# Cross-attention on one core: the last two blocks' subtraction split over VectorE and GpSimd, their inverse sums spread by DMA, their PSUM banks and step order changed

## The chip, the core and the metric

The kernel runs on one core of a Trainium2 chip. The metric is the device time of one execution in microseconds (us); lower is better. Engines are named as in the profile: PE (TensorE), DVE (VectorE), ACT (ScalarE), POOL (GpSimd), and SP, whose queue issues nearly all DMAs.

## What is computed

The reference is a cross-attention layer in float32. 16 batches of 1024 rows of 512 features attend to 64 context rows each, with 16 heads of 32 features:

```python
xq  = ada_ln(x, cond, Wss_q)          # layernorm, then scale and shift from silu(cond)
xkv = ada_ln(ctx, cond, Wss_kv)
q = (xq @ Wq + bq)                    # 16 heads x 32
k, v = split(xkv @ Wkv + bkv)
scores = einsum("bqhd,bkhd->bhqk", q, k) / sqrt(32)
attn = softmax(scores, axis=-1)
out = einsum("bhqk,bkhd->bqhd", attn, v)
return x + (out @ Wp + bp)
```

## The kernel before

The 16 x 1024 rows are cut into 32 blocks of 512 rows (`NB = 32`, two to a batch). Queries, scores and results are held transposed, features over the 128 partitions. The three 512x512 products use a seven-product scheme (Strassen's kind): `query_product(i, n)` and `product(i, n)` are the seven products of the query projection and of the output projection, and `added(i, n)` adds each product's accumulator to the residual rows `r`.

A block passes these steps, each of them a helper:

- `scores(i, z)`: PE makes the scores of context half `z` (0 or 1) in two PSUM pairs `ps`; DVE takes the column maxima into `m`, ACT copies the scores to the SBUF tile `s` (128x2048).
- `maxima(i)`: DVE joins the maxima of both halves and spreads them with a 32x32 block transpose to `mb` (128x2048). `subtract(i)`: POOL forms `s - mb`, once for each half. `weights(i, z)`: ACT takes the exponential in place.
- The sums: `total` (POOL adds the halves) and `row_total` (DVE), or, for the last block, `sums(i, z)` on DVE for each half and `halves_total`. `inverse_rows(i)`: DVE takes the reciprocal of the small 128x64 tile `lt`; SP writes it to a DRAM tile `ltd` and reads it back rearranged in four small DMAs to `vr` (128x64). `spread_rows(i)`: DVE spreads `vr` by a block transpose to `vb` (128x2048).
- `mix(i)`: PE multiplies the exponentials with the values into the PSUM tiles `po`; half 0 comes first. `divided(i)`: DVE forms `ot = po * vb`.
- The output projection: `biased` (ACT puts the bias into the PSUM accumulators `pp`), `row_sums` (POOL forms the sums of `ot` that the seven products need), seven `product`s on PE and seven `added`s on DVE, and the DMAs of the result out.

The program calls these helpers in an order written out by hand; every engine runs its own instructions in that order, and semaphores hold an instruction until what it needs is there. A loop handles the blocks up to 29; the *way out*, a written list after it, handles the last two, called `y` (block 30) and `z` (block 31). In the way out block 29 (`y - 1`) is projected without the seven products: `project(y - 1, t)` for four row tiles `t`, each of four PE instructions into one PSUM bank, and `projected(y - 1, t)`, which adds it to the rows on DVE and stores them.

Four PSUM banks (0 to 3) serve the projections. `ring` is the list from which `project` takes its bank in turn, `ks` in `mix(y - 1, ks=(2, 3, 1, 0))` are the banks of the four `po` tiles of block 29, and `acc_bank(i, n)` gives the banks of the accumulators. A bank that is taken again is held until the last reader of its old content is done. The other four banks are the two pairs in which the scores and the `po` of `y` and `z` stand in turn. Bank numbers before: `ring = [1, 0]`; block 30's accumulators are in banks 2 and 3 (its second product in 1), block 31's in 0 and 1 (its second product in 3).

## Time and profile before

| | |
|---|---|
| time, median of 3 runs | 1018.12 us (1017.64 to 1018.77) |
| time of the profiled execution, and its span | 1018.0 us, 1016.1 us |
| PE busy | 1002.6 us, 99% of the span |
| DVE, POOL, ACT busy | 861.7 us (85%), 809.3 us (80%), 638.5 us (63%) |
| granted PE clock | full speed over the span, but for the last few us |

The profile is of one execution. Its times run from the span's start; the way out begins near 940 us. In the timeline a row is a group of equal instructions: start, length, engine, line, operation, output<-inputs, count, and in square brackets how long the engine sat idle before it and who ended that. Ends of PE's groups are modelled, and a group's length reaches a little past the start of the next one.

### The profile page before, as it was taken

Reading aid. Unit: us, or ns where it says so; the run is one execution under the profiler, and the core shown is the slowest. Engines: PE = TensorE matmul, PEld = TensorE weight load, DVE = VectorE, ACT = ScalarE, POOL = GpSimd, SP = SyncE. Lnnn points to the kernel's source line nnn. Section 1 sums busy time; section 2 is a strip of 40 time slices with the busy share of each in tenths; the row PEclk is TensorE's granted clock in tenths of the full one; section 3 lists DMA queues with packets and bytes.
Section 4 is the critical chain, followed back from the end, with each engine's and each line's share of the span. In section 5 each row is a group of like instructions: output and inputs, shape, how many; then the busy total and the mean of one; then the engine's idle time right before and its main releaser. Section 6 shows DMA issues by size and latency. Waiting matters only on the chain.

```text
span 1016.1 us, 21264 instructions
## 1 busy us (share of the span) xinstructions
PE 1002.6 (99%) x8096; PEld 766.6 (75%) x8096; DVE 861.7 (85%) x1184; ACT 638.5 (63%) x1025; POOL 809.3 (80%) x518
## 2 busy tenths in 40 slices
PE   7999999999999999999999999999999999999998
PEld 6888777777777777777777777877777777777746
DVE  6687888898889888988898888889888888876785
ACT  3787566666667666666666666766666666665520
POOL 3668998888898888888988888898888888987781
PEclk9999999999999999999999999999999999999999
DMA  9664564444455544444554354444544444335122
GB/s 301 250 173 126 145 195 133 123 137 149 156 155 164 168 127 128 128 153 151 160 167 138 120 167 126 149 161 158 167 134 123 150 131 156 116 122 169 44 77 96
DMA packets 112101, 149.82 MB, mean 147 GB/s; under 512 B 34008, under 2 KB 45296, under 8 KB 112000
## 3 DMA queue, kind: packets, MB, share of 16 engines
q1 hardware_dynamic: 111600, 147.69, 46.9%
q8 instruction: 64, 1.05, 0.4%
q0 software_dynamic: 256, 0.52, 0.2%
q14 instruction: 37, 0.30, 0.1%
q10 hardware_dynamic: 144, 0.26, 0.1%
HBM read 79.21 MB, written 34.60 MB: 112 GB/s over the span
## 4 chain that ended last, share of the span: by engine, by line
PE 89%; DMA 3%; DVE 2%; POOL 2%; SPq 2%; issue 1%; ACT 1%; DVEq 0%; POOLq 0%; ACTq 0%
PE pq L551 36%; PE pp L964 35%; PE po L838 7%; PE ps L670 6%; PE pp L865 1%; PE pv_B L551 1%; PE pk_B L551 1%; SPq L398 1%; DMA x<-in_x_dram 1%; DMA w_v_sb<-in_L_xcond_Wkv_dram 1%; DMA b_v_sb<-in_L_xcond_bkv_dram 1%; PE pv_A L551 1%; POOL s L729 1%; DVE m L687 1%; POOL sum L769 0%
## 5 line engine op out<-in xcount | busy, mean ns | idle before, releaser
L729 POOL TENSOR_TENSOR s<-s,mb 128x2048 f32<-128x2048 f32 x64 | 290.5, 4565 | 124.3 <-DVE mb L716 124.3
L696 ACT COPY s<-ps 128x1024 f32<-128x1024 f32 x128 | 129.6, 1012 | 103.9 <-DVE m L687 61.7
L687 DVE TRANSPOSE_TENSOR_REDUCE m<-ps 128x32 f32<-128x1024 f32 x128 | 150.7, 1214 | 31.9 <-PE ps L670 31.9
L964 PE MATMUL pp<-w_p_sb,ot 128*128 128x256 f32 x736 | 169.1, 379 | 1.3 <-DVE ot L818 0.9
L987 DVE TENSOR_TENSOR r<-pp,r 128x512 f32<-128x512 f32 x210 | 136.7, 671 | 29.9 <-PE pp L964 24.5
L964 PEld LDWEIGHTS pp<-w_p_sb,ot 128*128 128x128 f32 x736 | 139.7, 190 | 21.3 <-issue 1.7
L590 ACT ACTIVATE qt<-pq,bias_t 128x256 f32<-128x256 f32 x256 | 105.7, 464 | 78.6 <-PE pq L551 78.5
L735 ACT ACTIVATE s<-s 128x2048 f32<-128x2048 f32 x64 | 122.3, 1913 | 47.3 <-POOL s L729 47.3
L769 POOL TENSOR_TENSOR sum<-s,s 128x2048 f32<-128x2048 f32 x31 | 140.7, 4540 | 3.1 <-ACT s L735 3.1
L964 PEld LDWEIGHTS pp<-WT,s 128*128 128x128 f32 x496 | 89.5, 189 | 57.8 <-issue 26.8
L551 PE MATMUL pq<-xt_sums,w_q_sums 128*128 128x256 f32 x512 | 123.7, 385 | 0.0
L964 PE MATMUL pp<-WT,s 128*128 128x256 f32 x496 | 123.1, 391 | 0.5 <-DVE r L987 0.5
L551 PEld LDWEIGHTS pq<-xt_sums,w_q_sums 128*128 128x128 f32 x512 | 95.0, 190 | 35.2 <-issue 22.5
L551 PE MATMUL pq<-xt,w_q_sb 128*128 128x256 f32 x512 | 121.3, 380 | 0.0
L551 PE MATMUL pq<-xt,w_q_sums 128*128 128x256 f32 x512 | 121.0, 379 | 0.0
L964 PE MATMUL pp<-WT,ot 128*128 128x256 f32 x496 | 117.3, 379 | 0.0
L551 PEld LDWEIGHTS pq<-xt,w_q_sb 128*128 128x128 f32 x512 | 97.0, 190 | 15.6 <-issue 1.7
L551 PEld LDWEIGHTS pq<-xt,w_q_sums 128*128 128x128 f32 x512 | 97.2, 190 | 13.3
L964 PEld LDWEIGHTS pp<-WT,ot 128*128 128x128 f32 x496 | 94.2, 190 | 13.6 <-issue 0.8
L347 ACT ACTIVATE x<-x,rstdq 128x512 f32<-128x512 f32 x128 | 97.1, 808 | 3.1 <-POOL rstdq L322 3.1
L456 ACT ACTIVATE xt<-xt,ss_q 128x512 f32<-128x512 f32 x124 | 94.1, 808 | 2.3 <-DMA out_dram<-r 1.3
L304 DVE BATCH_NORM_STATS2 bs<-x 128x6 f32<-128x512 f32 x128 | 87.1, 680 | 4.1 <-DMA x<-in_x_dram 4.1
(174 smaller groups left out, 1481.0 us busy)
## 6 DMA issues: line engine op xcount, KB each, us to landing
x<-in_x_dram SPq DMA_DIRECT2D x32, 1024.0 KB, 5.4
r<-in_x_dram SPq DMA_DIRECT2D x32, 1024.0 KB, 5.3
xt<-ht SPq DMA_DIRECT2D x488, 64.0 KB, 2.0
out_dram<-r SPq DMA_DIRECT2D x60, 512.0 KB, 3.7
wss_kv<-in_L_xcond_Wss_kv_dram SPq DMA_DIRECT2D x4, 512.0 KB, 8.3
wss_q<-in_L_xcond_Wss_q_dram SPq DMA_DIRECT2D x4, 512.0 KB, 8.0
vr<-ltd SPq DMA_DIRECT2D x128, 8.0 KB, 1.6
out_dram<-r SPq DMA_DIRECT2D x7, 256.0 KB, 2.3
```

Source lines behind the costliest of these rows:

```text
L304: nc.vector.bn_stats(bs, r)
L347: nc.scalar.activation(dst, src, AF.Identity, bias=rstd[:, 1, j : j + 1], scale=rstd[:, 0, j : j + 1])
L456: nc.scalar.activation(xt[:, :, c, :], xt[:, :, c, :], AF.Identity, scale=ss["q"][:, c, b : b + 1], bias=ss["q"][:, NC + c, b : b + 1],)
L551: nc.tensor.matmul(out_, lhsT=lhsT, rhs=rhs, start=new and m == 0 and c == 0, stop=c == HC - 1, skip_group_check=True,)
L590: nc.scalar.activation(dst, src, AF.Identity, bias=bq_t[:, o : o + 1])
L687: nc.vector.tensor_reduce(m_tiles[i][:, z, 2 * e : 2 * e + 2, :], s_banks[i, z][e].rearrange("p r (j a) -> p r j a", a=32), AX.X, ALU.max, ...
L696: nc.scalar.copy(s_tiles[i, z][:, 2 * e : 2 * e + 2, :], s_banks[i, z][e])
L729: eng.tensor_tensor(s_tiles[i, z], s_tiles[i, z], mb_tiles[i], ALU.subtract)
L735: nc.scalar.activation(p, p, AF.Exp, scale=SCALE)
L769: nc.gpsimd.tensor_tensor(t, s_tiles[i, 0], s_tiles[i, 1], ALU.add)
L964: nc.tensor.matmul(acc[products_of(i, n)][:, t * HO : (t + 1) * HO], lhsT=rows[:, c, t * P : (t + 1) * P], rhs=cols[:, c, :], start=n == 2 ...
L987: nc.vector.tensor_add(r, a, r)
```

## The change

The change concerns the way out alone; the 30 blocks before it are issued as before. Lines after it stand 15 to 17 lines later in the file where a helper moved.

```diff
+    def inverse_spread(i, lt):
+        turned_lt = small.tile([P, 2, 32], F32, tag="vr", name=f"vr_{i}")
+        nc.vector.transpose(turned_lt.rearrange("p h a -> p (h a)"), lt)
+        d = dram.tile([2, NC, 32, 32], F32, tag="lt", name=f"ltd_{i}")
+        nc.sync.dma_start(d.rearrange("h c x a -> (c x) h a"), turned_lt)
+        t = qpool.tile([P, NC, TB], F32, tag="vb", name=f"vb_{i}", bufs=1)
+        for r in range(HPC):
+            row = d[r // 2].rearrange("c (r j) a -> r c (j a)", r=2)[r % 2]
+            nc.sync.dma_start(
+                t[32 * r : 32 * r + 32], row.unsqueeze(0).to_broadcast([32, NC, TB])
+            )
+        vb_tiles[i] = t
+
     def inverse_rows(i):
         lt = lt_tiles.pop(i)
         nc.vector.reciprocal(lt, lt)
+        if i >= NB - 2:
+            inverse_spread(i, lt.rearrange("p r j -> p (r j)"))
+            return
...
     def acc_bank(i, n):
         if n == 2 and i >= NB - 2:
-            return 1 if i == NB - 2 else 3
-        return (2 if n in (1, 6, 5, 3) else 3) - (2 if i == NB - 1 else 0)
+            return 2 if i == NB - 2 else 1
+        return (2 if n in (1, 6, 5, 3) else 3) - (2 if i == NB - 2 else 0)
...
-    ring[:] = [1, 0]
+    ring[:] = [2, 3]
...
-    subtract(z)
+    subtract(z, nc.vector, (1,))
...
+    subtract(z, zs=(0,))
...
-    spread_rows(y)
...
-    spread_rows(z)
```

For blocks 30 and 31 the small tile of inverse sums is turned on DVE, written to DRAM, and read back by four DMAs, each of which fills 32 partitions of the full tile `vb` (256 KB each, 1 MB together) by reading the same rows 32 times. `subtract` of block 31 is made by DVE for half 1 and by POOL for half 0. Project tiles 0 to 3 of block 29 go to banks 2, 3, 2, 3 in place of 1, 0, 1, 0; block 30's accumulators to 0 and 1 (second product 2), block 31's to 2 and 3 (second product 1).

The steps of the way out stand in a new order; three places follow. On PE, from the projection of block 29 on (`pp_29`), before:

```order
L865 MATMUL pp_29_0_8778<-w_p_sb_102,ot_29_8744 128x512 x4
L865 MATMUL pp_29_1_8797<-w_p_sb_102,ot_29_8744 128x512 x4
L865 MATMUL pp_29_2_8804<-w_p_sb_102,ot_29_8744 128x512 x4
L838 MATMUL po_30_0_8818<-s_30_0_8572,V_B_123 32x512 x8
L838 MATMUL po_30_1_8819<-s_30_0_8572,V_B_123 32x512 x8
L838 MATMUL po_30_0_8818<-s_30_1_8606,V_B_123 32x512 x8
L838 MATMUL po_30_1_8819<-s_30_1_8606,V_B_123 32x512 x8
L865 MATMUL pp_29_3_8853<-w_p_sb_102,ot_29_8744 128x512 x4
L964 MATMUL pp_30_1_8746<-w_p_sb_102,ot_30_8858 128x256 x4
L964 MATMUL pp_30_2_8870<-w_p_sb_102,ot_30_8858 128x256 x4
L838 MATMUL po_31_0_8879<-s_31_0_8697,V_B_123 32x512 x8
```

and after:

```order
L882 MATMUL pp_29_0_8788<-w_p_sb_102,ot_29_8744 128x512 x4
L882 MATMUL pp_29_1_8802<-w_p_sb_102,ot_29_8744 128x512 x4
L855 MATMUL po_30_0_8809<-s_30_0_8572,V_B_123 32x512 x8
L855 MATMUL po_30_1_8810<-s_30_0_8572,V_B_123 32x512 x8
L855 MATMUL po_30_0_8809<-s_30_1_8607,V_B_123 32x512 x8
L855 MATMUL po_30_1_8810<-s_30_1_8607,V_B_123 32x512 x8
L882 MATMUL pp_29_2_8843<-w_p_sb_102,ot_29_8744 128x512 x4
L882 MATMUL pp_29_3_8848<-w_p_sb_102,ot_29_8744 128x512 x4
L855 MATMUL po_31_0_8863<-s_31_0_8703,V_B_123 32x512 x8
L855 MATMUL po_31_1_8864<-s_31_0_8703,V_B_123 32x512 x8
```

Block 30's `mix` now stands between project tiles 1 and 2, and block 31's `mix` (`po_31`, half 0 first) follows project tile 3 at once; block 30's first two products, which stood before it, come after it.

On DVE, from block 30's row sums (`lt_30`) to block 30's division, before:

```order
L774 TENSOR_REDUCE lt_30_8776<-sum_30_8702 128x64
L878 TENSOR_TENSOR r_29_8436<-pp_29_0_8778,r_29_8436 128x512
L789 RECIPROCAL lt_30_8776<-lt_30_8776 128x64
L707 TENSOR_REDUCE m_31_8793<-m2_31_8696 128x64
L716 STREAM_TRANSPOSE mb_31_8795<-m_31_8793 128x2048
L878 TENSOR_TENSOR r_29_8436<-pp_29_1_8797,r_29_8436 128x512
L800 STREAM_TRANSPOSE vb_30_8813<-vr_30_8786 128x2048
L878 TENSOR_TENSOR r_29_8436<-pp_29_2_8804,r_29_8436 128x512
L818 TENSOR_TENSOR ot_30_8858<-po_30_0_8818,vb_30_8813 128x1024
```

and after:

```order
L774 TENSOR_REDUCE lt_30_8753<-sum_30_8682 128x64
L687 TENSOR_REDUCE m2_31_8702<-ps_31_1_0_8755 128x32
L687 TENSOR_REDUCE m2_31_8702<-ps_31_1_1_8756 128x32
L803 RECIPROCAL lt_30_8753<-lt_30_8753 128x64
L789 STREAM_TRANSPOSE vr_30_8779<-lt_30_8753 128x64
L895 TENSOR_TENSOR r_29_8436<-pp_29_0_8788,r_29_8436 128x512
L707 TENSOR_REDUCE m_31_8795<-m2_31_8702 128x64
L716 STREAM_TRANSPOSE mb_31_8797<-m_31_8795 128x2048
L729 TENSOR_TENSOR s_31_1_8773<-s_31_1_8773,mb_31_8797 128x2048
L895 TENSOR_TENSOR r_29_8436<-pp_29_1_8802,r_29_8436 128x512
L895 TENSOR_TENSOR r_29_8436<-pp_29_2_8843,r_29_8436 128x512
L835 TENSOR_TENSOR ot_30_8856<-po_30_0_8809,vb_30_8783 128x1024
```

The row sums go ahead of block 31's last two maxima, the large transpose to `vb` is gone, a small one to `vr` is new, and the subtraction of half 1 stands ahead of the addition that empties project tile 1's bank.

On POOL, in the same stretch, before:

```order
L729 TENSOR_TENSOR s_30_0_8572<-s_30_0_8572,mb_30_8625 128x2048
L729 TENSOR_TENSOR s_30_1_8606<-s_30_1_8606,mb_30_8625 128x2048
L769 TENSOR_TENSOR sum_30_8702<-s_30_0_8572,s_30_1_8606 128x2048
L365 TENSOR_TENSOR r_29_8436<-r_29_8436,b_p_sb_101 128x512 x4
L729 TENSOR_TENSOR s_31_0_8697<-s_31_0_8697,mb_31_8795 128x2048
L729 TENSOR_TENSOR s_31_1_8771<-s_31_1_8771,mb_31_8795 128x2048
```

and after:

```order
L365 TENSOR_TENSOR r_29_8436<-r_29_8436,b_p_sb_101 128x512 x4
L729 TENSOR_TENSOR s_30_0_8572<-s_30_0_8572,mb_30_8635 128x2048
L729 TENSOR_TENSOR s_30_1_8607<-s_30_1_8607,mb_30_8635 128x2048
L769 TENSOR_TENSOR sum_30_8682<-s_30_0_8572,s_30_1_8607 128x2048
L729 TENSOR_TENSOR s_31_0_8703<-s_31_0_8703,mb_31_8797 128x2048
```

The bias additions to block 29's rows (`residual(y - 1)`) move ahead of block 30's subtraction, and one subtraction of block 31 is gone. In the list of steps at the end, block 31's `added(z, 2)` and its DMA move from after the fifth product to after the third.

84 lines of the change are left out of this document (42 added, 42 removed).

## The prediction

> **What bounds the kernel now.** I read the page first (engines, chain), then PE's timeline of the way out, then those of DVE, POOL, ACT and SP in the same window. The page's rows of busy time and of the chain that ended last:
>
> ```profile
> PE 1002.6 (99%) x8096; PEld 766.6 (75%) x8096; DVE 861.7 (85%) x1184; ACT 638.5 (63%) x1025; POOL 809.3 (80%) x518
> PE 89%; DMA 3%; DVE 2%; POOL 2%; SPq 2%; issue 1%; ACT 1%; DVEq 0%; POOLq 0%; ACTq 0%
> ```
>
> PE is the bound. The change removes no matmul, so it can only win time in which PE stands still in the way out. PE's timeline there:
>
> ```profile
> 965.72 1.25 PE L670 MATMUL ps<-qt,K_B 32*32 32x512 f32 x32
> 967.65 10.57 PE L865 MATMUL pp<-w_p_sb,ot 128*128 128x512 f32 x24 [0.68 <-DVE ot L813]
> 978.14 2.35 PE L838 MATMUL po<-s,V_B 32*32 32x512 f32 x64
> 996.79 1.89 PE L964 MATMUL pp<-WT,ot 128*128 128x256 f32 x8
> 999.58 1.97 PE L964 MATMUL pp<-w_p_sb,ot 128*128 128x256 f32 x8 [0.90 <-DVE ot L818]
> 1001.91 1.97 PE L964 MATMUL pp<-w_p_sb,ot 128*128 128x256 f32 x8 [0.36 <-DVE r L987]
> 1003.71 1.89 PE L964 MATMUL pp<-WT,s 128*128 128x256 f32 x8
> 1010.62 1.89 PE L964 MATMUL pp<-WT,ot 128*128 128x256 f32 x8
> ```
>
> From 1003.71 to 1010.62 four products start, so a product takes (1010.62 - 1003.71)/4 = 1.73 us; the 1.89 of a row reaches into the next one. Measured from start to start, PE loses three pieces: 0.68 ahead of project tile 0; 999.58 - (996.79 + 1.73) = 1.06 ahead of block 31's first product; 1001.91 - (999.58 + 1.73) = 0.60 ahead of its second. That is 2.34 us, 0.23% of the time: the most that the edit can win in PE's stream. After PE's last product, 1010.62 + 1.73 = 1012.35, follow an addition and a DMA out to the end of the span at 1016.1; these 3.7 us stay, for the last step is the same in both orders. A change under 0.2%, 2.0 us, is about what a measurement of this kernel cannot tell from none.
>
> DVE in the same stretch, where the three waits end:
>
> ```profile
> 965.75 2.45 DVE L813 TENSOR_TENSOR ot<-po,vb 128x512 f32<-128x512 f32 x4
> 968.11 2.36 DVE L687 TRANSPOSE_TENSOR_REDUCE m<-ps 128x32 f32<-128x1024 f32 x2
> 970.40 2.27 DVE L774 TRANSPOSE_TENSOR_REDUCE lt<-sum 128x64 f32<-128x2048 f32 x1
> 972.59 0.65 DVE L878 TENSOR_TENSOR r<-pp,r 128x512 f32<-128x512 f32 x1
> 973.17 0.53 DVE L789 RECIPROCAL lt<-lt 128x64 f32<-128x64 f32 x1
> 973.88 2.31 DVE L716 STREAM_TRANSPOSE mb<-m 128x2048 f32<-128x2048 f32 x1
> 983.68 2.29 DVE L740 TRANSPOSE_TENSOR_REDUCE l<-s 128x64 f32<-128x2048 f32 x1
> 989.71 0.29 DVE L707 TENSOR_REDUCE lt<-l 128x64 f32<-128x128 f32 x1
> 990.04 0.55 DVE L789 RECIPROCAL lt<-lt 128x64 f32<-128x64 f32 x1
> 995.88 2.30 DVE L800 STREAM_TRANSPOSE vb<-vr 128x2048 f32<-128x2048 f32 x1
> 998.21 2.36 DVE L818 TENSOR_TENSOR ot<-po,vb 128x1024 f32<-128x1024 f32 x2
> ```
>
> Block 31's inverse sums set the 1.06: reciprocal at 990.04, the way through DRAM, the transpose at 995.88, the division at 998.21. What they wait for ahead of that is POOL's two subtractions in a row, then ACT's exponentials; SP's rows give the price of the write to DRAM:
>
> ```profile
> 967.80 4.94 POOL L365 TENSOR_TENSOR r<-r,b_p_sb 128x512 f32<-128x512 f32 x4
> 976.34 9.05 POOL L729 TENSOR_TENSOR s<-s,mb 128x2048 f32<-128x2048 f32 x2 [3.60 <-DVE mb L716]
> 999.58 1.27 POOL L935 TENSOR_TENSOR s<-ot 128x512 f32<-128x512 f32 x1 [9.01 <-DVE ot L818]
> 980.92 1.91 ACT L735 ACTIVATE s<-s 128x2048 f32<-128x2048 f32 x1 [9.40 <-POOL s L729]
> 990.62 0.32 SPq L792 DMA_DIRECT2D ltd<-lt  x1
> 992.10 1.74 SPq L794 DMA_DIRECT2D vr<-ltd  x4
> ```
>
> **The change, part by part.** I walk the new order with these durations, on the clock of the profiled execution, from the point where PE finishes block 31's scores, 965.72 + 1.25 = 967.0.
>
> *Banks of block 29's projection.* Project tile 0 took bank 1, that of `po_2`, and so waited for DVE's third multiplication, 965.75 + 3 x 0.61 = 967.6. Bank 2 is that of `po_0`, free after the first, 966.4, before PE comes. The 0.68 goes. Block 30's accumulators now lie where `po_3` and `po_2` lay, so ACT's two bias copies wait until 968.2; ACT has 9.40 us idle ahead of its exponential at 980.92, which hides it.
>
> *Residual moved on POOL.* The 4.94 us now stand ahead of block 30's subtraction and are gone from 967.80, where POOL was about to idle 3.60 anyway:
>
> ```profile
> 952.20 9.03 POOL L729 TENSOR_TENSOR s<-s,mb 128x2048 f32<-128x2048 f32 x2 [5.17 <-DVE mb L716]
> ```
>
> POOL idles 5.17 ahead of that subtraction, so the 4.94 fit. Costed at nothing; without that cover the later exponentials of block 30, and the scores after them, would be late by what sticks out.
>
> *Moved query steps and additions.* They change places within DVE's and ACT's slack ahead of 962; the same products reach PE. Costed at nothing.
>
> *Project tiles 0 and 1, mix, tiles 2 and 3.* A tile takes 10.57/3 = 3.5 us, a mix 2.3. PE: tiles 0 and 1 to 974.0, block 30's mix to 976.3, tile 2 to 979.8. Tile 3 wants bank 3, which holds tile 1 until DVE adds it, and that addition now stands behind the large transpose and the new subtraction. DVE: the four multiplications to 968.1, row sums 2.27, two maxima 2.36, reciprocal 0.53, the small transpose (128x64; not in the trace; between the 0.29 of the small reduction and the 0.53 of the reciprocal on the same tile, I take 0.3), addition 0.65, joining the maxima 0.29, transpose 2.31: `mb` stands at 976.8. The subtraction on DVE is not in the trace with 2048 elements: from 2.29 (one input of that size) to 2.7 (four times the 0.68 quoted next). I take 2.3, since the fixed part of an instruction is paid once: 979.1. Addition 0.65: 979.8. With the passing of a semaphore tile 3 starts near 980.0: +0.2 (0.6 at the other end).
>
> *Two engines on one subtraction.* Both wait for `mb`, so both start together, each with two SBUF inputs. The only place where DVE instructions with two SBUF inputs run beside POOL is the start of the program:
>
> ```profile
> 20.64 0.68 DVE L507 TENSOR_TENSOR xk_A<-xk_A 128x512 f32<-128x512 f32 x1
> 21.35 1.64 DVE L507 TENSOR_TENSOR xk_sums_A<-xk_A 128x512 f32<-128x512 f32 x1
> 20.66 1.78 POOL L481 TENSOR_TENSOR w_k_sums<-w_k_sb 128x512 f32<-128x512 f32 x1
> 22.52 1.59 POOL L481 TENSOR_TENSOR w_k_sums<-w_k_sums,w_k_sb 128x512 f32<-128x512 f32 x1
> ```
>
> One of that shape takes 0.68 on DVE and 1.27 on POOL when alone. DVE's at 20.64 began first and kept its 0.68, while POOL's took 0.51 longer; DVE's at 21.35 came second and took 0.96 longer, to 22.99, which is 0.55 after POOL's ended; POOL's next ended 1.12 after that. They take turns, and the first keeps the lane to its end. [...]
>
> Here DVE comes first: it follows its own `mb` (995.88 + 2.30 to 998.21 is 0.03 between dependent instructions), while POOL started 0.15 after `mb` (973.88 + 2.31 to 976.34). POOL's half 0 then begins in earnest at 979.1 and ends at 979.1 + 9.05/2 - 0.15 = 983.5; its exponential 1.91 ends at 985.4. Block 31's mix, which takes half 0 first, finds PE free after tile 3 at 980.0 + 3.5 = 983.5 and starts at 985.5: +2.0, a new wait. Side by side, POOL would end at 981.5 and the exponential at 983.4: no wait.
>
> *Inverse sums as full tiles.* The two large transposes leave DVE (2.3 us each); in their place come the small transpose, a write (990.62 to 992.10, 1.48) and four reads of 256 KB into 32 partitions each. Their landing, R from the first issue, is the unknown. The page's DMA rows:
>
> ```profile
> r<-in_x_dram SPq DMA_DIRECT2D x32, 1024.0 KB, 5.3
> xt<-ht SPq DMA_DIRECT2D x488, 64.0 KB, 2.0
> out_dram<-r SPq DMA_DIRECT2D x60, 512.0 KB, 3.7
> vr<-ltd SPq DMA_DIRECT2D x128, 8.0 KB, 1.6
> out_dram<-r SPq DMA_DIRECT2D x7, 256.0 KB, 2.3
> ```
>
> Low end: 5.3, 1 MB as one DMA over all partitions. High end: the 32-partition rows, 8 KB in 1.6 and 64 KB in 2.0, give 0.4 per 56 KB, so 1.6 + 1016/56 x 0.4 = 8.9. From 256 to 512 KB a DMA takes 1.4 longer, so four of 256 KB one behind the other give 2.3 + 3 x 1.4 = 6.5, which I take as the row of nearest size.
>
> [...] No row here shows these reads.
>
> With R = 6.5, block 30: small transpose done at 973.5, read issued at 975.2, landed 981.7, divided (2.36) at 984.1. The mix of block 31 needs those PSUM banks only at 985.5: hidden. Block 31: sums of half 1 to 986.4, of half 0 to 988.7, then 0.29, 0.55 and 0.3 to 989.9; write to 991.4, landed 997.9, first half divided 999.1, second 1000.3. PE: mix 985.5 to 987.8, block 30's seven products to 999.9. So the first product waits for nothing: the 1.06 goes. The second wants bank 1, emptied by the addition after the division, 1000.9, against 1001.6: the 0.60 goes. POOL's three sums (1.27 each) end at 1003.2; the third product is due at 1003.4. The spare is 0.2 to 0.8 us. Behind the reads on SP stand the stores of tiles 0 to 2 and block 30's residual load, which has until 990; behind block 31's, stores alone. Above R = 6.8 each us costs two: one at block 30's division, which holds up block 31's sums on DVE, and one at block 31's own reads.
>
> **Sum.** -0.68 - 1.06 - 0.60 + 0.2 + 2.0 = -0.1 us. On the profiled execution's 1018.0 that is 1017.9; the median of the runs lies 0.1 higher, so 1018.0.
>
> **Rivals.**
> - *The subtractions do run side by side* (against: the rows at 20.64 to 22.52), and R is 5.3 to 5.6. Then the 2.0 is not paid: -2.1, 1016.0. With R = 6.5 and no turn-taking, block 30's division at 984.1 and block 31's reads bind instead, and the result is my forecast's. Chance 0.13.
> - *Long reads*, slower than before: if R = 7.8, past 6.8 by 1.0, +2 us (1020); at 8.9, +4.2 (1022.2). It decides for slower from R = 7.8. For it: the 32-partition rows; against: each of the 64 KB rows carries a fixed part that I may have spread over too few bytes. Chance of R over 7.2: 0.17.
> - *POOL gets the lane first.* DVE, blocked until 981.5, subtracts to 983.8, adds at 984.4, and tile 3 waits 4.8 in place of 0.2, while the 2.0 vanishes: +2.5, 1020.5. Against: the 0.03 and 0.15 above. Chance 0.06.
> - *The new order meets a wait that I have not seen* (a tile still read, a store ahead of a load): 0.5 to 4 us. Chance 0.04.
>
> **How the numbers follow.** My forecast (turns, DVE first, R from 5.3 to 7.2) holds 0.60 and spans -0.8 to +0.9, since errors of a few tenths sit on six terms: 1017.3 to 1018.9. The range of 8 in 10 takes in most of the first rival and the long reads up to R of about 8: 1016.1 to 1020.6. Faster by over 0.2%: half of the first rival and a little of the forecast's edge, 0.09. Slower by over 0.2%: half of the long reads, the third rival, half of the last, 0.18. Within: 0.73.
>
> **What would show it.** Right: no idle ahead of project tile 0; ahead of block 31's mix some 2 us that end on ACT; DVE's subtraction at 2.3, POOL's at about 6.6 from the same start; no wait at block 31's first product; `vb` landing 6 to 7 us after its first issue. Wrong: POOL's subtraction at 4.5 beside DVE's; DVE's at over 6; `vb` over 7.8.

## The result, and the profile after

The changed kernel takes 1018.96 us (median of 22 runs, 1017.97 to 1020.77), the kernel before 1017.58 us (22 runs, 1016.10 to 1018.77): ratio 1.0018, 95% interval 1.0011 to 1.0024: slower by 1.4 us in the medians, by 1.1 to 2.4 by the interval. The forecast was 1018.0, no change. The time lies inside the forecast's range of 1016.1 to 1020.6, but the interval leaves no room for "no change". The prediction took 2.0 us for the least that a measurement of this kernel can tell; 22 runs of each kernel give the difference to 0.7 us on either side.

The changed kernel's profiled execution took 1018.6 us, its span 1016.8. PE's timeline of the way out (start, duration, tile, count, idle time ahead):

```profile
964.79 1.25 PE L670 MATMUL ps<-qt,K_B 32*32 32x512 f32 x32
965.97 7.13 PE L882 MATMUL pp<-w_p_sb,ot 128*128 128x512 f32 x16
973.04 2.35 PE L855 MATMUL po<-s,V_B 32*32 32x512 f32 x64
975.32 7.13 PE L882 MATMUL pp<-w_p_sb,ot 128*128 128x512 f32 x16
984.35 2.71 PE L855 MATMUL po<-s,V_B 32*32 32x512 f32 x64 [1.90 <-ACT s L735]
987.00 3.72 PE L981 MATMUL pp<-w_p_sb,ot 128*128 128x256 f32 x16
991.04 1.97 PE L981 MATMUL pp<-WT,s 128*128 128x256 f32 x8 [0.32 <-DVE r L1004]
...
998.02 1.89 PE L981 MATMUL pp<-WT,ot 128*128 128x256 f32 x8
1000.41 3.69 PE L981 MATMUL pp<-w_p_sb,ot 128*128 128x256 f32 x16 [0.50 <-DVE ot L835]
1004.32 1.99 PE L981 MATMUL pp<-WT,s 128*128 128x256 f32 x8 [0.21 <-POOL s L956]
...
1011.33 1.89 PE L981 MATMUL pp<-WT,ot 128*128 128x256 f32 x8
```

A measure that leaves out the earlier parts of the program is PE's last stretch, from the start of block 31's second score products (L670) to the end of the last product (its start + 1.73). Before it is 1010.62 + 1.73 - 965.72 = 46.63 us; now it is 1011.33 + 1.73 - 964.79 = 48.27: +1.64, which is within the interval of the runs.

The 0.68 ahead of project tile 0 is gone (965.97 follows the scores at once). Five losses have come instead. Two project tiles take 973.04 - 965.97 = 7.07, so the mix was due at 982.39 and starts at 984.35: 1.96. The mix takes 987.00 - 984.35 = 2.65 where block 30's takes 2.28: 0.37. The third product is 0.58 late (991.04 - 987.00 - 2 x 1.73), block 31's first 0.66 (1000.41 - 998.02 - 1.73), its third 0.45. Together 4.0 against the 2.34 of before: +1.7. The 1.96 ends on ACT, behind POOL's subtraction. The other four, 2.1 together, stand behind the two divisions: by their brackets they end on block 31's division, on a POOL sum of what it gives, and on a DVE addition that is queued behind block 30's division and the sums; the 0.37 has no bracket and fits the end of block 30's division at 984.71, which empties the banks that the mix fills.

The timelines of POOL and ACT show the subtractions' turns (POOL's takes 6.64 us beside DVE's; before, POOL alone took 9.05 for two) and the exponentials behind them:

```profile
975.71 6.64 POOL L729 TENSOR_TENSOR s<-s,mb 128x2048 f32<-128x2048 f32 x1 [8.80 <-DVE mb L716]
```

```profile
978.00 1.91 ACT L735 ACTIVATE s<-s 128x2048 f32<-128x2048 f32 x1 [5.21 <-DVE s L729]
982.39 1.91 ACT L735 ACTIVATE s<-s 128x2048 f32<-128x2048 f32 x1 [2.47 <-POOL s L729]
```

DVE's shows the two divisions (L835) that wait for `vb`, and the sums behind the first:

```profile
975.67 2.29 DVE L729 TENSOR_TENSOR s<-s,mb 128x2048 f32<-128x2048 f32 x1
...
982.36 2.35 DVE L835 TENSOR_TENSOR ot<-po,vb 128x1024 f32<-128x1024 f32 x2 [2.61 <-DMA vb<-ltd]
984.63 4.49 DVE L740 TRANSPOSE_TENSOR_REDUCE l<-s 128x64 f32<-128x2048 f32 x2
...
999.04 2.36 DVE L835 TENSOR_TENSOR ot<-po,vb 128x1024 f32<-128x1024 f32 x2 [1.85 <-DMA vb<-ltd]
```

SP's has the first issue of the four reads of each block (L795), with block 30's residual load (L126, 1 MB) behind the first four; a store stands between:

```profile
974.06 1.76 SPq L795 DMA_DIRECT2D vb<-ltd  x4
...
976.40 0.39 SPq L126 DMA_DIRECT2D r<-in_x_dram  x1
...
991.97 1.76 SPq L795 DMA_DIRECT2D vb<-ltd  x4
```

From the first issue to the division: block 30 982.36 - 974.06 = 8.3 us, block 31 999.04 - 991.97 = 7.1. The prediction took 6.5 for both. The list of the instructions on `vb` has what a single read of 256 KB takes from its own issue, 3.3 at the least:

```profile
DMA to landing us min/median/max: 3.3/5.3/6.3
```

The list of waits puts the new one first among those of the way out that end on a DMA (total, times, longest):

```profile
DVE ot L835 <- DMA vb<-ltd: 4.5, 2, 2.6
```

### The profile page after: what moved, and what is told of

Read it like the earlier page. It is cut to its first block, busy times and chain, and to the rows that moved or that the text cites. A ratio compares the mean times of both kernels' runs of the same rounds, so it can differ in the third digit from the quotient of the medians.

```text
span 1016.8 us, 21267 instructions
## 1 busy us (share of the span) xinstructions
PE 1002.7 (99%) x8096; PEld 766.3 (75%) x8096; DVE 861.5 (85%) x1185; ACT 638.6 (63%) x1025; POOL 806.2 (79%) x517
## 3 DMA queue, kind: packets, MB, share of 16 engines
q8 instruction: 64, 1.05, 0.4%
## 4 chain that ended last, share of the span: by engine, by line
PE 86%; DVE 4%; DMA 3%; POOL 2%; SPq 1%; issue 1%; ACT 0%; DVEq 0%; POOLq 0%
PE pq L551 36%; PE pp L981 34%; PE ps L670 6%; PE po L855 6%; PE pv_B L551 1%; PE pk_B L551 1%; DMA vb<-ltd 1%; PE pk_A L551 1%; PE pv_A L551 1%; SPq L398 1%; DVE m L687 1%; DMA x<-in_x_dram 1%; POOL s L729 1%; DVE ot L835 1%; POOL sum L769 0%
```

## The experiments

My theory after the result: the four reads of `vb` are longer than I took them, and their length counts nearly twice, through block 30's division, behind which block 31's sums queue on DVE, and through block 31's own division. The first rival: taking turns on the subtraction is the whole cause. All runs in one table; "stretch" is PE's last stretch in the profiled execution, "landing" the time from the first issue of the reads to the division where that waits for them (block 30 / block 31), "low clock" the executions whose mean granted clock was 0.998 or less (TensorE's clock, 1 being full; among the executions of the kernel before listed beside the experiments there is none).

| kernel | ratio to before (95%) | stretch | landing | low clock |
|---|---|---|---|---|
| before | 1 | 46.63 | | 0 |
| changed | 1.0018 (1.0011 to 1.0024) | 48.27 | 8.3 / 7.1 | 11 of 22 |
| old sums | 1.0006 (0.9997 to 1.0015) | 47.50 | | 0 of 11 |
| DVE both | 1.0018 (1.0009 to 1.0027) | 48.03 | 8.1 / 7.1 | 1 of 11 |
| load apart | 1.0014 (1.0005 to 1.0023) | 48.67 | 7.8 / 8.0 | 7 of 11 |
| wide reads | 1.0136 (1.0122 to 1.0150) | 60.22 | 14.9 (30) | 4 of 4 |
| other rows | 1.0002 (0.9993 to 1.0011) | 47.68 | 8.2 (30) | 3 of 11 |
| all partitions | one run, 1018.1 | 46.17 | | 0 of 1 |
| sums first | 1.0009 (0.9999 to 1.0020) | 49.74 | 8.4 (30) | 2 of 11 |
| sums first, old 31 | 0.9999 (0.9990 to 1.0008) | 46.66 | | 1 of 11 |
| banks only | one run, 1018.9 | 46.15 | | 0 of 1 |
| filled | 1.0015 (1.0006 to 1.0024) | 48.52 | 8.1 / 7.5 | 0 of 11 |
| old sums exchanged | 1.0005 (0.9996 to 1.0014) | 46.94 | | 0 of 11 |
| POOL both | 1.0028 (1.0016 to 1.0040) | 48.77 | 8.2 / 7.5 | 6 of 6 |
| two queues | 1.0010 (1.0001 to 1.0018) | 47.95 | 8.3 / 6.6 | 7 of 11 |
| two queues, old 31 | 1.0012 (1.0003 to 1.0021) | 47.24 | 8.4 (30) | 2 of 11 |
| the same, load apart | 0.9997 (0.9988 to 1.0006) | 46.77 | 7.9 (30) | 0 of 11 |

The intervals are 0.9 us wide on each side, so the difference of two of these kernels is known to some 1.1 us on either side, and smaller steps are read from the profiles, one execution each. The profiled executions of wide reads, other rows, sums first, POOL both and two queues are themselves of low clock, so their stretches hold its price too. Other rows and all partitions divide by rows of the input and not by the sums: what they give out for blocks 30 and 31 is not the layer's result.

### Old sums: the reads taken away

```diff
 def inverse_rows(i):
-        if i >= NB - 2:
-            inverse_spread(...)
-            return
...
     project(y - 1, 1)
+    spread_rows(y)
     mix(y)
...
     added(y, 5)
+    spread_rows(z)
     divided(z)
```

> The changed kernel, with the inverse sums of blocks 30 and 31 brought back by small tiles and a DVE transpose as in the kernel before; order, banks and split subtraction stay. Long reads (my theory): the time lost against the changed kernel's 4.0 us of waits starts at vb. Without the reads, block 30's small tiles land by 977.6, the transpose fits into DVE's 2.6 us of idle time, and block 30's division starts 0.8 us earlier; block 31's way from reciprocal to division takes 7.6 instead of 9.6 us. The waits ahead of block 30's third product and of block 31's first products go: -1.5 to -2.0 us against the changed kernel, which is -0.1 to -0.6 against the kernel before. Turn-taking alone (rival): the 1.9 us ahead of block 31's mix is all that counts, and it stays: 0 against the changed kernel, +1.4 against before. Both keep an idle time of about 1.9 us ahead of the mix that ends on ACT.

Ratio 1.0006: some 1.2 us less than the changed kernel, give or take 1.1; that is short of the theory's 1.5 to 2.0 and only just clear of the rival's 0. The stretch is 0.8 shorter. PE waits 1.62 for ACT ahead of the mix, as expected, and 0.9 ahead of block 31's product:

```profile
1001.79 3.69 PE L978 MATMUL pp<-w_p_sb,ot 128*128 128x256 f32 x16 [0.90 <-DVE ot L832]
```

The second wait is of my own making: I put block 31's transpose (998.08) behind the addition of product 5, which itself waited 1.03 for PE; SP had issued the last of the small reads by 995.1. So this run does not show what small tiles cost when the transpose is well placed; "sums first, old 31" below does.

### DVE both: the turns taken away

```diff
-    subtract(z, nc.vector, (1,))
+    subtract(z, nc.vector, (0,))
     load_residual(y)
     project(y - 1, 1)
+    subtract(z, nc.vector, (1,))
...
-    subtract(z, zs=(0,))
...
-    weights(z, 1)
-    sums(z, 1)
     weights(z, 0)
+    weights(z, 1)
+    sums(z, 1)
```

> The changed kernel, with both of block 31's subtractions on DVE, half 0 first, so that nobody takes turns; half 0's exponential goes first. Long reads: exponentials end at about 979.9 and 982.8, so ACT no longer holds the mix; but the mix now waits for block 30's division, which waits for vb (982.4) as before, and DVE's sums follow the same division: the mix ends at most 0.5 us earlier, block 31's products start at the same time: 0 to -0.3 us against the changed kernel. Turn-taking alone: the 1.9 us ahead of the mix go, -1.9 us against the changed kernel, -0.5 against before.

Ratio 1.0018, as the changed kernel, where the rival asked for 1.9 us less: the rival is out. The exponentials (on ACT, first fence) end at 980.1 and 982.9, yet the mix starts no earlier than block 30's division lets it, and block 31's product not at all:

```profile
978.18 1.91 ACT L735 ACTIVATE s<-s 128x2048 f32<-128x2048 f32 x1 [5.21 <-DVE s L729]
980.98 1.91 ACT L735 ACTIVATE s<-s 128x2048 f32<-128x2048 f32 x1 [0.89 <-DVE s L729]
```

```profile
982.35 2.35 DVE L835 TENSOR_TENSOR ot<-po,vb 128x1024 f32<-128x1024 f32 x2 [0.80 <-DMA vb<-ltd]
```

```profile
983.72 3.33 PE L855 MATMUL po<-s,V_B 32*32 32x512 f32 x64 [1.09 <-DVE ot L835]
...
1000.37 3.69 PE L981 MATMUL pp<-w_p_sb,ot 128*128 128x256 f32 x16 [0.48 <-DVE ot L835]
```

So the 2.0 that the prediction charged to turn-taking is real, but it hides a wait for block 30's division of nearly the same size: 1.09 ahead of the mix and 1.05 inside it (3.33 for 2.28). Taking one away leaves the other. Of that second wait 0.80 is shown to be `vb`'s, the idle time of DVE ahead of the division; until then DVE is busy with the second subtraction, which this run gave it.

### Load apart

```diff
     added(y - 2, 3)
+    load_residual(y)
     total(y)
...
-    load_residual(y)
```

> The changed kernel, with block 30's residual load (1 MB) issued on SP ahead of the write and the reads of block 30's inverse sums instead of right behind them. Long reads with shared DMA engines: block 30's reads, 8.2 us with the load behind them, fall to the 7.0 us that block 31's take alone; block 30's division and what DVE does after it come 1.2 us earlier; the waits ahead of block 30's third product and block 31's first two products shrink or go: -1.2 to -2.0 us against the changed kernel. If the load has no part in it: the reads stay at 8.2 us, 0 us. Turn-taking alone: 0 us whatever the reads do.

Block 30's landing fell by 0.5 only, to 7.8, and block 31's, which the edit does not touch, was 8.0 in this execution: SP needed 2.86 us for its four issues instead of 1.76.

```profile
973.80 1.75 SPq L795 DMA_DIRECT2D vb<-ltd  x4
...
991.21 2.86 SPq L795 DMA_DIRECT2D vb<-ltd  x4
```

```profile
981.60 2.36 DVE L835 TENSOR_TENSOR ot<-po,vb 128x1024 f32<-128x1024 f32 x2 [2.15 <-DMA vb<-ltd]
...
999.16 2.36 DVE L835 TENSOR_TENSOR ot<-po,vb 128x1024 f32<-128x1024 f32 x2 [2.69 <-DMA vb<-ltd]
```

A miss: the 1.2 between the two blocks did not go, and since block 31's landing came out 0.9 longer without any edit, not even block 30's 0.5 is shown to be the load's. The time is that of the changed kernel.

### Wide reads, other rows, all partitions: why the reads are long

Three kernels ask whether it is the span of 32 partitions or the rows that all partitions repeat. First the same rows, each transfer over all 128 partitions:

```diff
-        d = dram.tile([2, NC, 32, 32], ...)
-        nc.sync.dma_start(d.rearrange("h c x a -> (c x) h a"), turned_lt)
+        d = dram.tile([NC, 2, 32, 32], ...)
+        for h in range(2):
+            nc.sync.dma_start(d[:, h], turned_lt[:, h, :])
...
+        for c in range(NC):
+            row = d[c].rearrange("h (r j) a -> (h r) (j a)", r=2)
+            nc.sync.dma_start(t[:, c, :], row.unsqueeze(1).to_broadcast([HPC, 32, TB]))
```

> The changed kernel, with the same 1 MB of vb read by four transfers that each span all 128 partitions (2 KB a partition, one chunk of 512 columns) instead of four that span 32 partitions each (8 KB a partition); the rows in DRAM are as many times repeated, the pieces as long (2 KB), and the write is split in two (+0.4 us). Long reads by the narrow span: the last lands about 5.3 us after the first issue, as the 1 MB loads over all partitions do, and the first two by 3.5; block 30's division then starts when DVE is free (about 980), and the waits behind it go: -1.5 to -2.0 us against the changed kernel, -0.1 to -0.6 against before. Long reads by repeated rows in DRAM (rival): the transfers stay at 7.0 to 8.2 us, only the first half comes earlier: 0 to +0.9 us against the changed kernel. Turn-taking alone: 0.

12 us slower than the changed kernel, far from every expectation. Block 30's division waits twice, and the second half lands 990.56 - 975.67 (first issue) = 14.9 us after the first issue. The stretch of block 31's reads (columns at the end: granted clock, DMA share, GB/s):

```profile
983.86 1.23 DVE L836 TENSOR_TENSOR ot<-po,vb 128x1024 f32<-128x1024 f32 x1 [3.62 <-DMA vb<-ltd]
990.56 1.23 DVE L836 TENSOR_TENSOR ot<-po,vb 128x1024 f32<-128x1024 f32 x1 [5.47 <-DMA vb<-ltd]
```

```profile
1002.00:1008.00 6.00, 6.00 (x29) 5.28 (x29) 2.83 (x5) 0.59 (x1) 0.96 (x1) 1.00 0.26 99
```

A share of 0.26 is four of 16 engines' worth of time, where the reads of the changed kernel have 1.06 (windows below). The outermost dimension of these transfers has size four; that this holds the share down is a guess of the author's, which no run shows by itself. With the engines idle three quarters of the time, the pace here is set by something else than in the changed kernel, so this run tells nothing of rows against span; the next two do.

```diff
+        rows = rows_of(x, i - 4)
         for r in range(HPC):
-            row = ...
-            nc.sync.dma_start(t[32 * r : 32 * r + 32], row...to_broadcast([32, NC, TB]))
+            nc.sync.dma_start(t[32 * r : 32 * r + 32], rows[32 * r : 32 * r + 32])
```

> The changed kernel, but the four reads of vb, as many, as large, into the same 32 partitions each and in pieces of the same 2 KB, fetch rows of the input x that all differ instead of rows of the small tile in DRAM that repeat 32 times. What is divided by is then not the sums: the output of blocks 30 and 31 is not the reference's. The reads also no longer wait for the write ahead of them, which brings them 1.2 us forward. Repeated rows are what is slow (the theory that the wide reads left standing: 14.9 us to the last landing there against 7.0 to 8.3): the reads take 5.3 us or less from the first issue; block 30's division starts when DVE is free for it (about 980), only the 1.9 us ahead of block 31's mix is left, and the kernel is 1.7 to 2.1 us faster than the changed one (-0.3 to -0.7 against before). Narrow span is what is slow (rival): the reads still take 7 to 8 us; the 1.2 us alone give -0.5 to -1.5.

Then, against the edit just shown, the same rows into all partitions:

```diff
-        for r in range(HPC):
-            nc.sync.dma_start(t[32 * r : 32 * r + 32], rows[32 * r : 32 * r + 32])
+        for c in range(NC):
+            nc.sync.dma_start(t[:, c, :], rows[:, c, :])
```

> As the run with other rows of x in place of the sums (so the output of blocks 30 and 31 is not the reference's), but each of the four reads spans all 128 partitions (one chunk of 512 columns, 2 KB a partition) instead of 32. Narrow span is what holds the rate at about 210 GB/s (what the run with other rows left standing): block 31's 1 MB moves at 350 GB/s or more, in about 3 us instead of 4.8, and lands some 5.3 us after the first issue. The DMA engines' own limit (rival): 210 GB/s as before.

One window each while block 31's reads run, of the changed kernel, of other rows, of all partitions:

```profile
994.00:997.00 3.00, 3.00 (x16) 2.64 (x15) 1.20 (x2) 0.00 (x0) 0.00 (x0) 1.00 1.06 210
```

```profile
993.00:996.00 3.00, 3.00 (x16) 2.65 (x15) 1.39 (x2) 0.59 (x1) 1.27 (x1) 1.00 1.07 212
```

```profile
992.00:994.00 2.00, 2.00 (x11) 1.76 (x10) 0.91 (x2) 0.59 (x1) 1.27 (x1) 1.00 1.02 381
```

210 and 212 GB/s into 32 partitions, repeated rows or not; 381 GB/s into all. The DMA engines are busy all the time in each (shares of 1.02 to 1.07). The narrow span nearly halves the rate; my expectation for other rows, that the repeated rows did it, was wrong. The first read of block 31 lands 3.3 us after its issue in the changed kernel, where the median of the eight reads is 5.3; in the run over all partitions that median is 2.9. 256 KB take 1.25 us at 210 GB/s and 0.69 at 381, so by these rates some 2.0 of the 3.3 and 2.2 of the 2.9 are left (an estimate). In the run over all partitions nothing is left but the wait for the exponential:

```profile
985.99 2.37 PE L853 MATMUL po<-s,V_B 32*32 32x512 f32 x64 [1.92 <-ACT s L735]
```

Its stretch, 46.17, is 0.46 under that of before: with short reads the prediction's sum (-0.1, of which the 0.2 for tile 3 did not come) is what the profile shows, though these reads, like those of other rows, also start 1.2 us earlier, and one profile does not part the two. Other rows gained 1.6 us on the changed kernel in the runs, give or take 1.1, with reads that came 1.2 us earlier and were no faster: it is the time at which `vb` comes that costs. Whether one us of landing counts for more than one of time is more than these intervals can tell.

### Two queues

```diff
         for r in range(HPC):
+            eng = (nc.sync, nc.scalar)[r // 2]
-            nc.sync.dma_start(...)
+            eng.dma_start(...)
```

> The changed kernel, with the four reads of vb issued from two queues, the first two on SP and the last two on ACT, which idles there. The low rate belongs to one transfer into 32 partitions, and transfers of one queue go one behind the other (theory): with two going at once block 31's 1 MB moves at up to 390 GB/s, as into all partitions, and lands some 5.2 us after the first issue instead of 7.0; block 30's, beside a store and a load, some 6.5 instead of 8.3. Only the 1.9 us ahead of block 31's mix is left: -1.3 to -2.1 us against the changed kernel. The low rate belongs to all such transfers together (rival): 210 GB/s as before, the same landings, 0 us.

Block 31's landing is 6.6, block 30's 8.3 as before. The change in time, 0.8 us, is less than the two intervals resolve.

```profile
991.50 2.32 SPq L796 DMA_DIRECT2D vb<-ltd  x2
```

```profile
998.14 2.36 DVE L836 TENSOR_TENSOR ot<-po,vb 128x1024 f32<-128x1024 f32 x2 [0.50 <-DMA vb<-ltd]
```

So two narrow transfers at once gain half a microsecond here and not the factor of a wide one: the rival is nearer. The fullest window of 1 us has 322 GB/s here (995 to 996) and 287 with one queue (993 to 994 in the changed kernel). The test is weaker than it was meant to be, for SP's two issues took 2.32 us for block 31 where they took 0.80 for block 30, so the second pair started late; why is not shown. What block 30's reads still wait for beside load and store was tried in the last run below.

### Filled: the clock behind the idle time

```diff
     projected(y - 1, 2)
+    warm = bank("warm_z", 2)
+    for _ in range(12):
+        nc.tensor.transpose(warm[:, :P], ident, ident)
```

> The changed kernel, with 12 transposes of a 128x128 tile (0.14 us each, 1.7 us) put on TensorE behind project tile 3, where it idles 1.9 us ahead of block 31's mix; nothing else moves. The clock falls where PE stands still (new theory: in half of the changed kernel's executions the mean granted clock is 0.998 or less, in none of the kernel before's): the executions with 0.998 or less go, the median falls by about 0.5 us, the upper group of times (1019.4 to 1020.8) thins out. The clock has nothing to do with that idle time (rival): as many executions with 0.998 or less, and the same median within 0.2 us.

```profile
982.67 1.47 PE L1593 MATMUL warm_z<-ident 128*128 128x128 f32 x12
```

No execution has the low clock any more (0 of 11 against 11 of 22): with the gap filled it did not come. The length of the gap alone does not decide it, for old sums, with 1.62 idle ahead of the mix, has it in 0 of 11. The ratio hardly moved, 1.0015 against 1.0018: the half microsecond that I expected is not shown. In the changed kernel the 11 executions of low clock have a median of 1019.45, the other 11 of 1018.53; the groups overlap (1018.4 to 1020.8 and 1018.0 to 1020.5), so the clock is a part of the spread and not the whole. The 11 without it still lie 0.95 above the median of the kernel before, so it is not the clock alone that makes the changed kernel slower.

The profile of two queues is of low clock and shows how it can cost so little. One window and the mix:

```profile
984.00:988.00 4.00, 4.00 (x64) 1.26 (x64) 4.00 (x3) 0.00 (x0) 3.04 (x3) 0.57 0.04 13
```

```profile
983.91 4.18 PE L856 MATMUL po<-s,V_B 32*32 32x512 f32 x64 [1.90 <-ACT s L735]
```

A mean of 0.57 over 4 us is 3.4 us at 0.50, the clock of the window 988 to 992 in the next section (an estimate), and the mix takes 4.18 in place of the 2.71 of the changed kernel's profile. But PE, some 1.5 late, then waits for nothing: the delay takes the place of the waits that stood behind the mix. That this holds in the low-clock executions of the changed kernel too is argued, for none of them was profiled.

### Sums first, and block 31 by small tiles

```diff
-    subtract(z, nc.vector, (1,))
+    subtract(z, nc.vector, (0,))
...
-    subtract(z, zs=(0,))
+    subtract(z, zs=(1,))
     projected(y - 1, 2)
+    weights(z, 0)
+    sums(z, 0)
     divided(y)
     weights(z, 1)
     sums(z, 1)
-    weights(z, 0)
     mix(z)
     product(y, 1)
-    sums(z, 0)
```

> The changed kernel, with the halves exchanged (DVE subtracts half 0, which the mix takes first, POOL half 1) and block 31's sums of half 0 put on DVE ahead of block 30's division, where DVE idles 2.6 us waiting for vb. If the long reads cost through DVE's queue (my theory): half 0's exponential ends at 979.9, its sums run to 982.2 in the idle time, the division stays at 982.4, the sums of half 1 end at 987.0 instead of 989.1, so the second reads start 2.2 us earlier and block 31's division comes at about 997 instead of 999.0; the mix starts at 983.6 instead of 984.35. PE then loses 1.1 to 1.6 us ahead of and inside the mix and nothing behind it: -1.7 to -2.4 us against the changed kernel, -0.3 to -1.0 against before. Turn-taking as the only cause (rival): the mix's second half still waits for POOL's half, 984.4: -0.5 at most.

Nine of 11 executions lie from 1016.95 to 1018.86, the two of low clock at 1021.0 and 1021.9, the profiled one among these: 0.9 us under the changed kernel by the ratio, 1.5 by the medians, where 1.7 to 2.4 was expected. The windows and PE rows of the profiled execution show what a low clock costs when it comes: mix 4.40 and two products 5.86, against 3.34 and 3.72 in the profile of the next run.

```profile
984.00:988.00 4.00, 3.26 (x61) 1.09 (x64) 3.97 (x4) 1.21 (x1) 3.23 (x3) 0.82 0.48 180
988.00:992.00 4.00, 4.00 (x22) 2.44 (x8) 1.02 (x3) 0.00 (x0) 0.56 (x1) 0.50 0.10 25
992.00:996.00 4.00, 4.00 (x16) 3.38 (x16) 1.39 (x2) 0.35 (x1) 0.97 (x1) 0.83 1.03 229
```

```profile
984.70 4.40 PE L855 MATMUL po<-s,V_B 32*32 32x512 f32 x64 [1.34 <-DVE ot L835]
989.02 5.86 PE L981 MATMUL pp<-w_p_sb,ot 128*128 128x256 f32 x16
...
1003.35 3.62 PE L981 MATMUL pp<-w_p_sb,ot 128*128 128x256 f32 x16
```

Nothing waits behind the mix any more (1003.35 follows the product before it at once). That fits the theory's second path, but a PE made 3.2 us late by its clock would find `vb` there in any case; the next run's profile, at full clock, lists no wait behind the mix either, with block 31 on small tiles. Then the same with block 31's inverse sums by small tiles, the transpose ahead of the addition after product 5:

```diff
-        if i >= NB - 2:
+        if i == NB - 2:
             inverse_spread(...)
...
     product(y, 5)
+    spread_rows(z)
     product(y, 4)
```

> The kernel of the run before (halves exchanged, sums of half 0 first), with block 31's inverse sums by small tiles and the DVE transpose again, the transpose put ahead of the addition after product 5; block 30 keeps the reads of full tiles. My theory: block 31's way from reciprocal to vb is then 7.6 us instead of 8.9, landing in DVE's gaps, so block 31's division is ready some 2 us before PE wants it, and PE loses nothing behind the mix even where reads are slow in an execution: -2.0 to -2.9 us against the changed kernel, -0.6 to -1.5 against before. If the reads of block 31 cost nothing once the sums come early: the same as the run before.

```profile
983.50 3.34 PE L855 MATMUL po<-s,V_B 32*32 32x512 f32 x64 [1.06 <-DVE ot L835]
```

Ratio 0.9999: 1.9 us under the changed kernel, where 2.0 was expected at the least, and level with the kernel before, not under it. What is left, 1.1 ahead of the mix for block 30's division and 1.0 inside it (3.3 for 2.28), is about what the kernel before lost in its three waits.

### Banks only

The bank numbers of the change in the kernel before, nothing else (`ring[:] = [2, 3]` and the new `acc_bank`).

> The kernel before, with the exchange of PSUM banks alone. By my prediction's sum: the 0.68 ahead of project tile 0 go and the kernel is 0.68 us faster. By the chain through DVE (rival): block 31's subtraction waits for mb, and DVE waited only 0.2 us for that tile's addition; so tile 0 starts 0.68 earlier, but the wait ahead of block 31's first product grows from 1.06 to 1.5 or more, and 0.0 to 0.2 us are won.

```profile
990.77 1.99 PE L964 MATMUL pp<-WT,s 128*128 128x256 f32 x8 [0.19 <-POOL s L939]
...
1000.58 1.96 PE L964 MATMUL pp<-w_p_sb,ot 128*128 128x256 f32 x8 [0.91 <-DVE ot L818]
```

Tile 0 starts with the scores' end (968.38, no idle time ahead). Some 0.25 come back at 990.77, ahead of block 30's third product, where PE now waits for POOL's sums; the waits ahead of block 31's first two products are as before (1.07 and 0.60). The stretch is 46.15: 0.48 won, and the first wait did not grow to the rival's 1.5, so the rival falls. The one time of this run says nothing at that size.

### Old sums exchanged, POOL both

Old sums with the halves exchanged (DVE half 0, POOL half 1, sums in that order):

```diff
-    subtract(z, nc.vector, (1,))
+    subtract(z, nc.vector, (0,))
...
-    subtract(z, zs=(0,))
+    subtract(z, zs=(1,))
...
```

> The kernel with the inverse sums of both blocks by small tiles and DVE transposes, and the halves exchanged: DVE subtracts half 0, POOL half 1, sums in that order. My theory: with the halves exchanged the mix starts on time at 982.5 by the changed kernel's clock, since half 0's exponential ends at 979.9 and block 30's division is no longer held by long reads; POOL's half is needed only 1.2 us later and is 0.7 late. PE loses 0.7 to 1.1 us in the mix instead of 1.9, and 0.7 to 1.0 ahead of block 31's first products, where the transpose and the division stand behind the sums: -0.8 to -1.3 us against the same kernel without the exchange, -0.2 to -0.7 against before. If the way from half 1 through its sums sets the end (rival): block 31's division comes no earlier, and the 1.1 won in the mix turn into waiting: 0 to -0.3 against the kernel without the exchange.

The mix starts on time (983.56, where project tile 3 ends), as expected; the wait of 0.9 ahead of block 31's first product is the one of the misplaced transpose. The stretch is 0.56 shorter than without the exchange, where 0.8 to 1.3 was expected; the ratios, 1.0005 and 1.0006, show no gain.

The changed kernel without the split (`subtract(z)` on POOL, half 0 first):

> The changed kernel without the split: both subtractions on POOL as before the change, half 0 first. POOL ends half 0 at 980.2 and half 1 at 984.8, the exponentials end at 982.1 and 986.7; the mix starts at 983.6 with block 30's division, its second half waits for 986.7 and it ends at 987.9 instead of 987.0; DVE's queue (division at 982.4, sums to 989.2) is as before, so block 31's division stays at 999.0. Long reads: the 0.9 us lost at the mix take the place of the waits ahead of block 30's third product and block 31's first: 0 to +0.4 us against the changed kernel, that is, the split wins next to nothing here. If the subtraction sets the end (rival): +0.9 us or more.

```profile
983.40 2.22 PE L855 MATMUL po<-s,V_B 32*32 32x512 f32 x32 [1.19 <-DVE ot L835]
986.47 2.02 PE L855 MATMUL po<-s,V_B 32*32 32x512 f32 x32 [0.84 <-ACT s L735]
```

1.0 us more than the changed kernel by the ratio (the intervals overlap), 0.5 in the stretch, and all six executions have the low clock. That is nearer the rival's number than mine. In this profile PE waits for nothing behind the mix, but its clock is low there (the two products behind the mix take 4.34 us, in the changed kernel 3.72), so whether the subtraction or the reads set the end is not shown. The split may be worth 0.5 to 1.0; how much of that is the clock stays open.

### The last two: can two queues make a gain of it

"Sums first, old 31" with block 30's reads from two queues and its division ahead of the sums of half 0; then with `load_residual(y)` ahead of the reads as well.

> The version with the halves exchanged, block 30 by full tiles and block 31 by small tiles, with block 30's reads from two queues (SP and ACT) and its division ahead of the sums of half 0. If two queues bring block 30's vb by 980: the division runs from 980 to 982, the mix starts on time at 982.5 instead of 983.5 and waits only for half 1's exponential (984.4); block 31's division has its sums at the same time as before: -0.8 to -1.1 us against the version without, as much against the kernel before. If the rate of both together stays at 210 GB/s: the division stands at 982.4 ahead of the sums, which end 0.2 later or more: 0 to +0.5 us against before.

> The run before (halves exchanged, block 31 by small tiles, block 30's reads from two queues, division first), with block 30's residual load issued ahead of those reads. If it was the load, now entering beside the reads of the second queue, that kept vb at 8.3 us: with two queues and no load the landing comes at some 6.3 us from the first issue, the division starts at 980, the mix on time at 982.5, and waits only for half 1: -0.8 to -1.1 us against before. If two narrow transfers at once move no faster than one (rival): the landing stays at 7.8 us, as with the load apart and one queue, the mix starts at 983.0: -0.5 to +0.5 us against before.

```profile
981.71 2.36 DVE L836 TENSOR_TENSOR ot<-po,vb 128x1024 f32<-128x1024 f32 x2 [2.73 <-DMA vb<-ltd]
```

```profile
983.11 2.36 DVE L836 TENSOR_TENSOR ot<-po,vb 128x1024 f32<-128x1024 f32 x2 [2.27 <-DMA vb<-ltd]
```

The division waits 2.73 and 2.27 for `vb`: two queues do not shorten the landing beside the stores (8.4 and 7.9 from first issues at 973.30 and 975.19), with or without the load. The first came out 1.3 us above the version it came from, the second level with the kernel before. No version here beats the kernel before by more than its interval.

## Why the prediction was wrong, step by step

- *Banks*: right. The 0.68 is gone in the changed kernel and alone wins 0.48.
- *Residual moved*: right; POOL's subtraction of block 30 follows it without a gap and no wait on PE came of it.
- *Tile 3 waits 0.2*: did not come; tiles 2 and 3 are back to back (975.32, 7.13 for both).
- *Turns, DVE first*: right in size. 2.29 on DVE and 6.64 on POOL from the same start (4.5 on POOL alone), 1.96 ahead of the mix against 2.0. That it is paid alone was not: "DVE both" shows the wait for block 30's division (983.7) right below it.
- *Inverse sums as full tiles*: the step that failed. It took R = 6.5 "as the row of nearest size", from stores over 128 partitions: 2.3 us for the first 256 KB and 1.4 for each of the other three. It measured 7.1 alone and 8.3 beside a load and a store. The rate was not the error: 256 KB in 1.4 us are 187 GB/s, and these reads moved at 210. Of block 31's 7.1 the first read takes 3.3 to land, 1.0 more than the row, and the other three 3.8 where the prediction put 4.2. Of the 1.0, some 0.6 is the narrow span by the rates (1.25 us for 256 KB at 210 GB/s, 0.69 at 381; an estimate); the rest is open. The 1.2 that block 30's reads take on top stay open too: a store and a load share their stretch, and neither "load apart" (7.8) nor two queues (8.3) took it away.
- *The 6.8 above which each us counts two*: no run shows it. As a bound it fits the prediction's own times, 6.5 and half of the 0.7 that are spare at block 31's second product (1001.6 - 1000.9), an estimate. What the runs showed in its place are landings of 7.1 to 8.4 with reads of the changed kernel's kind, and 6.6 for block 31 from two queues.
- *The slope*, one us at each block for each us above R = 6.8: right in kind, for block 30's division holds up the sums and block 31's division waits again. 8.3 and 7.1 give 1.5 + 0.3 = 1.8 on top of -0.1, +1.7; the profile has +1.64. That the two agree to a tenth is partly luck. By the prediction's own times the spare is 0.2 at block 31's third product and 0.8 at its first, and the two landings are 1.8 + 0.6 = 2.4 above 6.5, so its sum spans +1.5 to +2.1.
- The spare was 0.2 to 0.8 us for a term whose bounds were 5.3 to 8.9: the rival of long reads deserved far more than 0.17.
- What no part of the sum had: in half of the executions the mean granted clock is 0.998 or less, and with the idle time ahead of the mix filled in none. Its price in the ratio is not resolved ("filled").

## What to carry to other kernels

Price several DMAs in a row by the landing of the first and by what each further one adds, both from transfers of the same span and direction: stores over 128 partitions had 2.3 and 1.4 us, reads into 32 took 3.3 and some 1.3. Then ask what is issued right behind them. When two waits end within a few tenths of each other, taking one away wins nothing, so find the wait that stands below the one you remove. A step that relieves an engine by 4.6 us in exchange for a landing only pays if that landing has room, and room of under 1 us is none where landings vary by 0.9 from one execution to the next.

## What the runs showed of the hardware

- Reads into 32 partitions moved at 210 GB/s with repeated rows (the changed kernel) and at 212 with rows that all differ ("other rows"); into 128 partitions at 381 ("all partitions"). Two of the narrow ones at a time, from two queues, landed 0.5 us earlier at best (6.6 for 7.1, block 31).
- The first read of block 31, 256 KB into 32 partitions, landed 3.3 us after its issue in the changed kernel (median of the eight reads 5.3); in "all partitions" the median of the eight was 2.9.
- In "wide reads" transfers whose outermost dimension has size four moved at 99 GB/s with the DMA engines busy 0.26 of the time (block 31); 1 MB took 14.9 us from the first issue (block 30).
- After 1.34 us ("sums first") and 1.90 us ("two queues") of idle time ahead of the mix PE's granted clock fell, to 0.50 over 988 to 992 in the first and to a mean of 0.57 over 984 to 988 in the second. In the changed kernel's profile, after 1.90 us, it stayed at 1.00 over both windows. With 12 transposes in the gap none of 11 executions was of low clock, nor was one of old sums' 11, whose profile has 1.62 idle. Counted at 0.50, the low clock lasted 3.4 us in "two queues" (mean clock 0.998) and twice that in "sums first" (0.82, 0.50 and 0.83 over 4 us each, mean clock 0.997), an estimate.
